# A pause behind each gather, turned orders within tiles, and column lists with more whole blocks in a four-layer graph network

## The chip, the cores and the metric

The kernel runs on one core of a Trainium2 chip. The metric is the device time of one execution in microseconds (us). The core's engines work side by side, each through its own instruction queue in order: TensorE (PE, with its weight loads PEld), VectorE (DVE), ScalarE (ACT), GpSimd (POOL) and SyncE (SP, which here only issues DMAs). DMAs that GpSimd issues go through a software queue: GpSimd itself is busy for each of them.

## The reference

Four layers over 4096 nodes with 128 features. The adjacency matrix is 4096 x 4096 and sparse: the first nodes have many neighbours (hubs), the later ones few, and the diagonal is always set. Each layer normalizes x, takes the positive part h, and adds its result to x.

```python
def layer0(h): return h @ W_self.T + (adj @ h) @ W_neigh.T + b
def layer1(h):                                    # Chebyshev, K = 3
    t1 = adj @ h
    t2 = 2.0 * (adj @ t1) - h
    return h @ w[0] + t1 @ w[1] + t2 @ w[2] + bias
def layer2(h):                                    # attention
    H = h @ weight.T
    C = (H @ att_src)[None, :] + (H @ att_dst)[:, None]
    Tau = adj.T * exp(max(0.2 * C, C))
    return (adj.T * (Tau / Tau.sum(1, keepdims=True))) @ H
def layer3(h):                                    # messages
    s, d = h @ msg_w[:, :D].T, h @ msg_w[:, D:].T
    agg = einsum('ijd,ij->id', gelu(s[:, None] + d[None, :] + msg_b), adj)
    f = gelu(concat([h, agg], -1) @ upd_w.T + upd_b) + h
    return layernorm(f) * ln_w + ln_b
for layer in (layer0, layer1, layer2, layer3):
    x = x + layer(relu(layernorm(x)))
```

## The kernel before

The nodes are put into another order on the host (lines 62 to 81), so that the 32 blocks of 128 nodes hold similar numbers of entries. The kernel then uses the sparsity in two ways.

For layers 0 to 2 the matrix is cut into stripes: `ROWS`, 16 stripes of 256 rows of the matrix, and `COLS`, 16 stripes of 256 columns (class `Stripe`, line 84). A stripe has `near` blocks, which are read whole as 128x256 tiles, and a list for the rest: those nodes outside the near blocks that have any entry in the stripe, in `cap` chunks of 128 places. Line 102 chooses how many leading blocks are near: it takes the smallest of `len(near) + cap * (1 + extra)`, with `extra` 2 for rows and 1.5 for columns (line 119). Before the change the columns have 94 near blocks and 74 chunks in all, the rows 112 and 68.

A chunk costs gathers: GpSimd DMAs with an index for each partition, all issued by the helper `gather` (lines 552 to 554). For row stripes, `Layer.gather` (line 1102) gathers for each chunk the segment of the matrix (`rseg`, in layer 0 only; it is stored to `r_tab` for the other layers) and the nodes' features (`g`, from the tables h_tab of layer 0, h_tab of layer 1's input, and u_tab). For column stripes, `fetch_columns` (line 731) gathers segments into `cseg` and SP stores them to `c_tab`, and in attention `Attention.rows` (line 1208) gathers features from `a_tab`.

The last layer works on single entries. While the matrix is read (`read_adj`, `mark`, `scan`, lines 753 to 798), VectorE picks out the words that hold entries; `entries` (line 805) turns them into lists of 158 chunks of up to 128 entries, `values` (line 930) gathers each entry's value (`e_val`), and `Messages.rows` (line 1344) gathers d's row of each entry from `d_tab` into a tile of up to four chunks (the tiles are named m, and later halves of the tiles tau and e are used too).

The order of the work is written by a planner (class `Plan`, line 255). Every part of the kernel is a generator that yields what it needs next: a buffer, an event, or an engine with a time in microseconds. The planner keeps a clock for each engine, takes the piece of work that can begin first (ranks decide between those within `PATIENCE`), and the instructions are recorded in that order. `in_order` (line 348) then fixes the order on each engine. So the times that the generators yield (`GATHER`, line 376, for a gather on GpSimd) decide the order, and not what the chip does within it. `fill` (line 604) puts matmuls on a tile of zeros into TensorE's planned gaps. Buffers are given back with `plan.release`, at the planner's time; the least time is taken first.

Attention (`Attention.attend`, line 1215) works on units of up to four blocks or chunks of a column stripe. For each block ScalarE makes a biased positive part (line 1228), for the unit one exponential (line 1231), VectorE two multiplies by the matrix tile (lines 1235 and 1237), and TensorE for each block two products: the denominators (line 1252) and the numerators (line 1254). Adds on GpSimd, besides gathers, are the bias adds of lines 979 (128x1024) and 1000 (128x512).

Of the kernel before, what the change touches and what calls it, by code (L numbers as in the profile page):

```python
# [27 lines left out]
P = 128  # L28
# [3 lines left out]
GB = BANK // D  # L32
# [83 lines left out]


RS, CS = 256, 256
R_EXTRA, C_EXTRA = 2, 1.5
TOGETHER = GB * CS // RS  # L120
ROWS = [Stripe(i, RS, R_EXTRA) for i in range(N // RS)]
COLS = [Stripe(i, CS, C_EXTRA) for i in range(N // CS)]
# [250 lines left out]


SP = "SP", 0.07
GATHER = "POOL", 1.27


def sparse_stack(tc, x, adj, adjT, diag, w_self, w_neigh, b0, w1, b1, w2, att_src, att_dst,
# [10 lines left out]
    with ExitStack() as ctx:  # L390
# [7 lines left out]
        def kept(name, shape, dtype=F32):  # L398
            return keep.tile(list(shape), dtype, name=name, tag=name)
# [149 lines left out]
        junks = tiles(keep, "junk", 2, (P, D))  # L549
        aggs = tiles(keep, "agg", 2, (P, BANK))  # L550

        def gather(dst, table, index):
            nc.gpsimd.indirect_dma_start(out=dst, out_offset=None, in_=table[:, :],  # L553
                                         in_offset=bass.IndirectOffsetOnAxis(ap=index, axis=0))


        def norm(blocks, dst):
# [24 lines left out]
        def to_features(blocks, rows):  # L582

            n = blocks.stop - blocks.start
            p = yield banks
            yield "PE", 0.42 * n
            for k in range(n):
                nc.tensor.transpose(p[:, k * P:(k + 1) * P], rows[:, k, :], ident)
            yield on_act(n * P)
            nc.scalar.copy(hT[:, blocks.start * P:blocks.stop * P], p[:, :n * P])  # L590
            plan.release(banks, p)
# [11 lines left out]

        def fill(begin, time):

            idle = min((free, i, slots.items) for slots in (banks, picks) for free, i in slots.free + [(1e9, 0)])
            if idle[0] < begin - 1.0:
                for _ in range(int(time / 0.22)):
                    nc.tensor.matmul(idle[2][idle[1]], nothing[:, :P], nothing, start=True, stop=True)  # L609
# [455 lines left out]
        class Layer:  # L1065
# [58 lines left out]
            def multiply(self):  # L1124
                for g in range(NC):
                    bank = yield accs
                    for s in ROWS:
                        if s.lo // BANK != g:
                            continue
                        acc = bank[:, s.lo % BANK:s.lo % BANK + RS]  # L1130
                        count, every = 0, len(s.near) + s.cap
                        for i, blocks in enumerate(s.tiles(TOGETHER)):
                            yield self.near_here[s.index][i]
                            t = self.at["near", s.index, i]
                            for k, b in enumerate(blocks):
                                yield self.near_done[b // GB]
                                yield on_pe(RS)
                                nc.tensor.matmul(acc, self.near[:, b, :D], as_rows(t)[:, k, :], start=count == 0,  # L1138
                                                 stop=count == every - 1)
                                count += 1  # L1140
                            plan.release(bigs, t)
                        for i, chunks in enumerate(s.groups(TOGETHER)):
                            if self.number:
                                yield self.list_here[s.index][i]
                                t = self.at["list", s.index, i]
                            for k, c in enumerate(chunks):
                                yield self.rows_here[s.index][c]
                                row = self.at["row", s.index, c]
                                if self.number:
                                    r = as_rows(t)[:, k, :]  # L1150
                                else:
                                    r, here, left = self.at["seg", s.index, c]
                                    yield here
                                yield on_pe(RS)
                                nc.tensor.matmul(acc, row[:, :D], r, start=count == 0, stop=count == every - 1)  # L1155
                                count += 1
                                plan.release(rows_g, row)
                                if not self.number:
                                    left.set(plan.finish)
                            if self.number:  # L1160
                                plan.release(bigs, t)
                    agg = yield aggs
                    yield on_act(BANK)
                    nc.scalar.copy(agg, bank)
                    plan.release(accs, bank)
                    plan.start(self.finish(g, agg), -5)
                self.through.set(plan.finish)
# [6 lines left out]
        class Attention:  # L1174
# [40 lines left out]
            def attend(self, s, a, here, blocks, chunks, rows):  # L1215
                n = len(blocks or chunks)
                yield dst_done[s.lo // BANK]
                e = yield es_
                parts = []
                for k in range(n):  # L1220
                    if blocks:
                        yield a_done[blocks[k] // GB]
                        h = hB[:, blocks[k], :]
                    else:
                        yield rows[k][1]
                        h = rows[k][0]
                    yield on_act(CS + 100)
                    nc.scalar.activation(e[:, k, :], dst[:, s.lo:s.lo + CS], AF.Relu, bias=h[:, D:D + 1])
                    parts.append(h)
                yield on_act(n * CS, "exp")  # L1230
                nc.scalar.activation(e[:, :n, :], e[:, :n, :], AF.Exp, scale=0.8)  # L1231
                yield here
                tau = yield taus
                yield on_dve(n * CS)
                nc.vector.tensor_mul(tau[:, :n, :], e[:, :n, :], a[:, :n, :])  # L1235
                yield on_dve(n * CS)
                nc.vector.tensor_mul(e[:, :n, :], tau[:, :n, :], a[:, :n, :])
                plan.release(bigs, a)
                if s.index not in self.accs:
                    self.accs[s.index] = None  # L1240
                    self.accs[s.index] = yield accs
                    self.count[s.index] = 0
                while self.accs[s.index] is None:
                    yield acc_here[s.index]
                acc_here[s.index].set(0.0)
                every = len(s.near) + s.cap
                acc = self.accs[s.index]
                yield "PE", 0.4 * (self.count[s.index] == 0) + 2 * n * 0.65
                if self.count[s.index] == 0:
                    open_bank(acc)  # L1250
                for k in range(n):
                    nc.tensor.matmul(acc[0:1, CS:2 * CS], parts[k][:, D + 1:], tau[:, k, :], start=False, stop=False)
                for k in range(n):
                    nc.tensor.matmul(acc[:, :CS], parts[k][:, :D], e[:, k, :], start=False,
                                     stop=self.count[s.index] == every - 1)
                    self.count[s.index] += 1
                plan.release(taus, tau)
                plan.release(es_, e)
                for g, _ in rows:
                    plan.release(rows_g, g)  # L1260
                if self.count[s.index] == every:
                    plan.start(finish_3(s, acc), -5)
                    self.through.set(plan.finish)
# [52 lines left out]
        class Messages:  # L1316
# [27 lines left out]
            def rows(self, u, chunks, m, here):  # L1344
                groups = -(-4 * u.cuts[-1] // BANK)
                for g in range(groups):
                    yield d_here[g]
                for q, k in enumerate(chunks):
                    yield GATHER
                    n = u.within(k)  # L1350
                    gather(m[:n, q, :], d_tab[:groups * BANK, :], e_col[:n, k:k + 1])
                    here[q].set(plan.transfer(P * D * 4))

            def prepare(self, g):
# [21 lines left out]
                nc.scalar.activation(own, own, AF.Gelu)  # L1376
                r = yield r_tiles
                yield on_dve(BANK)
                for k in range(GB):
                    nc.vector.tensor_scalar(r[:, k, :], ident, diag_sb[:, g * GB + k:g * GB + k + 1], None, op0=ALU.mult)  # L1380
                self.acc[g] = acc = yield (accs if g else picks)
                yield "PE", 4 * 0.42
# [8 lines left out]
            def message(self, g, b, u, c, chunks, m, here):  # L1391
# [4 lines left out]
                yield self.s_here[g]  # L1396
                r = yield r_tiles
                yield "DVE", 0.35 * n
                for q, k in enumerate(chunks):
                    nc.vector.tensor_scalar(r[:, q, :], iota_row[:, :P], e_row[:, k:k + 1], e_val[:, k:k + 1],  # L1400
                                            op0=ALU.is_equal, op1=ALU.mult)
                for q in range(n):
# [584 lines left out]
```

## Time and profile before

| what | us |
|---|---|
| median of 14 runs (1191.1 to 1203.62) | 1198.99 |
| the profiled execution | 1191.22 |
| its span, first to last instruction | 1189.0 |
| TensorE busy in the span | 977.6 |
| VectorE busy | 793.3 |
| GpSimd busy | 773.9 |
| ScalarE busy | 672.5 |

The mean granted clock of TensorE is 0.933 of full speed. GpSimd's 773.9 us hold 736 gathers of 1.0 us on average. The first gather starts at 83 us and the last at 1138 us. By kind, in the order in which they begin: 68 of `rseg` (83 to 347 us), 136 from `h_tab` (101 to 495), 74 of `cseg` (329 to 575), 158 of `e_val` (502 to 921), 68 from `u_tab` (533 to 663), 74 from `a_tab` (734 to 930), and 158 from `d_tab` (921 to 1139).

How to read it: rows of the timeline are start, duration, engine, line, operation, out<-in, and in brackets the time for which the engine was idle before and what ended it; "issue" stands where the profile shows no releaser. Rows by stretch give the stretch, its length, the busy time with the count of instructions in brackets, TensorE's granted clock, the share of time in which the DMA engines were busy, and GB/s. All gathers have the line of the helper `gather`, so they are told apart by their tiles.

### The profile page before, as it was taken

Reading aid. Unit: us, or ns where it says so; the run is one execution under the profiler, and the core shown is the slowest. Engines: PE = TensorE matmul, PEld = TensorE weight load, DVE = VectorE, ACT = ScalarE, POOL = GpSimd, SP = SyncE. Lnnn points to the kernel's source line nnn. Section 1 sums busy time; section 2 is a strip of 40 time slices with the busy share of each in tenths; the row PEclk is TensorE's granted clock in tenths of the full one; section 3 lists DMA queues with packets and bytes.
Section 4 is the critical chain, followed back from the end, with each engine's and each line's share of the span. In section 5 each row is a group of like instructions: output and inputs, shape, how many; then the busy total and the mean of one; then the engine's idle time right before and its main releaser. Section 6 shows DMA issues by size and latency. Waiting matters only on the chain.

```text
span 1189.0 us, 19187 instructions
## 1 busy us (share of the span) xinstructions
PE 977.6 (82%) x5943; PEld 672.9 (57%) x5943; DVE 793.3 (67%) x2982; ACT 672.5 (57%) x1344; POOL 773.9 (65%) x832
## 2 busy tenths in 40 slices
PE   5878889888788888778879788989999997779860
PEld 2545566555546766667667554554555565657650
DVE  5789978798787868658768565555555733356652
ACT  4997667777413122223456575676878632455770
POOL 5115778455366777677777777777777757777720
PEclk9978989998888999889999899899999999999995
DMA  7999999999559778898766533444455222233310
GB/s 224 378 329 334 391 386 397 382 386 368 177 160 278 233 224 268 271 280 272 220 184 194 158 90 109 117 115 114 112 132 144 66 62 54 50 69 85 75 29 21
DMA packets 175416, 236.03 MB, mean 199 GB/s; under 512 B 22453, under 2 KB 155337, under 8 KB 167113
## 3 DMA queue, kind: packets, MB, share of 16 engines
q1 hardware_dynamic: 148904, 186.45, 46.3%
q0 software_dynamic: 26400, 48.27, 16.6%
q8 instruction: 49, 0.80, 0.3%
q14 instruction: 63, 0.51, 0.1%
HBM read 203.41 MB, written 31.23 MB: 197 GB/s over the span
## 4 chain that ended last, share of the span: by engine, by line
DMA 26%; PE 26%; DVE 16%; ACT 14%; POOL 9%; issue 7%; SPq 0%; POOLq 0%; DVEq 0%; ACTq 0%
POOL e_val L553 5%; PE acc L1138 5%; ACT mask L768 3%; DMA big<-in_adjT 3%; DMA dst<-in_adj 3%; DMA g<-h_tab,fetch_row 3%; ACT junk L568 3%; PE acc L1155 3%; DMA m<-d_tab,e_col 2%; DMA cseg<-in_adj,seg_col 2%; DMA e_val<-in_adj,e_at 2%; PE pick L609 2%; POOL g L553 2%; DMA g<-a_tab,fetch_col 2%; PE bank L597 2%
## 5 line engine op out<-in xcount | busy, mean ns | idle before, releaser
L553 POOL DMA_INDIRECT e_val<-in_adj,e_at x158 | 158.3, 1002 | 48.0 <-issue 41.3
L553 POOL DMA_INDIRECT g<-h_tab,fetch_row x136 | 134.3, 987 | 44.0 <-issue 27.3
L609 PE MATMUL pick<-nothing 128*128 128x512 f16 x532 | 135.4, 401 | 0.0
L609 PEld LDWEIGHTS <-nothing 128*128 128x128 f16 x795 | 80.5, 104 | 88.0 <-issue 17.6
L1138 PE MATMUL acc<-big,hA 128*128 128x256 f32 x448 | 119.1, 411 | 7.9 <-DMA big<-in_adjT 6.5
L553 POOL DMA_INDIRECT rseg<-in_adjT,seg_row x68 | 73.7, 1084 | 66.5 <-issue 35.0
L1138 PEld LDWEIGHTS acc<-big,hA 128*128 128x128 f32 x448 | 88.6, 207 | 22.8 <-DMA big<-in_adjT 7.7
L553 POOL DMA_INDIRECT cseg<-in_adj,seg_col x74 | 70.8, 957 | 42.0 <-issue 19.5
L553 POOL DMA_INDIRECT g<-a_tab,fetch_col x74 | 78.2, 1057 | 22.6 <-issue 14.3
L768 ACT ACTIVATE mask<-dst 128x2048 fp8e4<-128x2048 f32 x43 | 81.9, 1904 | 19.0 <-DMA dst<-in_adj 19.0
L1235 DVE TENSOR_TENSOR tau<-e,big 128x512 f32<-128x512 f32 (+3 forms) x61 | 54.3, 890 | 43.5 <-ACT e L1231 41.3
L553 POOL DMA_INDIRECT m<-d_tab,e_col x70 | 69.0, 986 | 21.3 <-issue 14.0
L553 POOL DMA_INDIRECT tau<-d_tab,e_col x63 | 61.2, 972 | 28.9 <-issue 12.2
L1155 PE MATMUL acc<-big,g 128*128 128x256 f32 x272 | 73.0, 402 | 8.2 <-DMA big<-r_tab 5.0
L553 POOL DMA_INDIRECT g<-u_tab,fetch_row x68 | 64.5, 948 | 20.7 <-issue 10.7
L1138 PE MATMUL acc<-big,hB 128*128 128x256 f32 x224 | 64.8, 430 | 13.9 <-DMA big<-in_adjT 13.9
L568 ACT ACTIVATE junk<-xN,stat 128x128 f32<-128x128 f32 x128 | 51.3, 401 | 41.9 <-DVE stat L564 29.5
L887 ACT COPY ehit<-pick 128x192 f32<-128x192 f32 (+7 forms) x74 | 20.3, 287 | 88.5 <-PE pick L884 75.2
L609 PE MATMUL bank<-nothing 128*128 128x512 f16 x263 | 67.4, 399 | 0.0
L1155 PE MATMUL acc<-rseg,g 128*128 128x256 f32 x136 | 44.1, 426 | 27.2 <-DMA g<-h_tab,fetch_row 27.0
L890 DVE SCALAR_TENSOR_TENSOR ehit<-ehit,pos,pick 128x32 f32<-128x32 f32 (+7 forms) x158 | 38.7, 284 | 39.1 <-ACT ehit L887 38.8
L622 ACT ACTIVATE sel_t<-iota_row,mids 128x512 f32<-128x512 f32 (+3 forms) x43 | 27.1, 641 | 60.7 <-DVE mids L617 60.1
(328 smaller groups left out, 2606.4 us busy)
## 6 DMA issues: line engine op xcount, KB each, us to landing
dst<-in_adj SPq DMA_DIRECT2D x43, 1024.0 KB
big<-in_adjT SPq DMA_DIRECT2D x45, 512.0 KB
raw<-in_adj SPq DMA_DIRECT2D x21, 1024.0 KB
big<-in_adjT SPq DMA_DIRECT2D x66, 256.0 KB
big<-r_tab SPq DMA_DIRECT2D x30, 512.0 KB
c_tab<-cseg SPq DMA_DIRECT2D x74, 128.0 KB
r_tab<-rseg SPq DMA_DIRECT2D x68, 128.0 KB
big<-c_tab SPq DMA_DIRECT2D x15, 512.0 KB
```

The costliest lines, as they stand in the source:

```text
L553: nc.gpsimd.indirect_dma_start(out=dst, out_offset=None, in_=table[:, :], in_offset=bass.IndirectOffsetOnAxis(ap=index, axis=0))
L568: nc.scalar.activation(junk, src[:, k, :], AF.Square, bias=st[:, 0, k:k + 1], accum_out=st[:, 1, k:k + 1])
L597: nc.tensor.matmul(p[:, k * D:(k + 1) * D], lhs[:, k * P:(k + 1) * P], w, start=i == 0, stop=i == len(terms) - 1)
L609: nc.tensor.matmul(idle[2][idle[1]], nothing[:, :P], nothing, start=True, stop=True)
L622: nc.scalar.activation(lane["t"][:, :n * P], iota_row[:, :n * P], AF.Abs, bias=mids[:, g:g + 1])
L768: nc.scalar.activation(mask[:, h * HALF:(h + 1) * HALF], raw_of[b, h], AF.Sigmoid, scale=1e38, accum_out=marks[:, 2 * b + h:2 * b + h + 1] ...
L887: nc.scalar.copy(hit, pv[:, :, :W])
L890: nc.vector.scalar_tensor_tensor(hit[:, q, :], hit[:, q, :], pos0[:, k + q:k + q + 1], pv[:, q, W:2 * W], op0=ALU.is_le, op1=ALU.mult, acc ...
L1138: nc.tensor.matmul(acc, self.near[:, b, :D], as_rows(t)[:, k, :], start=count == 0, stop=count == every - 1)
L1155: nc.tensor.matmul(acc, row[:, :D], r, start=count == 0, stop=count == every - 1)
L1235: nc.vector.tensor_mul(tau[:, :n, :], e[:, :n, :], a[:, :n, :])
```

## The change

It has four parts.

- Behind each gather, GpSimd adds the tile of ones to itself into a tile `pause` of 128x128 f32, which nothing reads. The planner's time for a gather goes from 1.27 to 1.52.
- `C_EXTRA` goes from 1.5 to 3. The columns then have 156 near blocks and 56 chunks (94 and 74 before): the first two stripes are whole (32 blocks each), the third has 10 blocks and 5 chunks, the others up to 11 blocks and 3 or 4 chunks. The rows are the same. With it 700 gathers remain of 736.
- Several loops over the parts of a tile run backwards: the transposes of four blocks in `to_features`, the attention products of a unit, the gathers of a message tile, and the making of the r tiles. Row buffers of a group are given back at the group's end, and in another order.
- `fill` compares only the first two members of its entries.

The planner runs with the new times and lists, so the order of the instructions differs on every engine from the first hundred on. In the sparse part TensorE has 6605 instructions shown for 6418, of them 881 idle-time matmuls for 811.

```diff
-R_EXTRA, C_EXTRA = 2, 1.5
+R_EXTRA, C_EXTRA = 2, 3
...
-GATHER = "POOL", 1.27
+GATHER = "POOL", 1.52
...
+        pause = kept("pause", (P, P))
+
         def gather(dst, table, index):
+
             nc.gpsimd.indirect_dma_start(out=dst, out_offset=None, in_=table[:, :],
                                          in_offset=bass.IndirectOffsetOnAxis(ap=index, axis=0))
+            nc.gpsimd.tensor_add(pause, ones, ones)
...
-            for k in range(n):
+            for k in reversed(range(n)):
                 nc.tensor.transpose(p[:, k * P:(k + 1) * P], rows[:, k, :], ident)
...
-            idle = min((free, i, slots.items) for slots in (banks, picks) for free, i in slots.free + [(1e9, 0)])
+            idle = min(((free, i, slots.items) for slots in (banks, picks) for free, i in slots.free + [(1e9, 0)]),
+                       key=lambda slot: slot[:2])
...
                                 count += 1
-                                plan.release(rows_g, row)
                                 if not self.number:
                                     left.set(plan.finish)
+                            for k, c in enumerate(reversed(chunks)):
+                                plan.release(rows_g, self.at["row", s.index, c], plan.finish + 1e-6 * k)
...
-                for k in range(n):
+                for k in reversed(range(n)):
                     nc.tensor.matmul(acc[0:1, CS:2 * CS], parts[k][:, D + 1:], tau[:, k, :], start=False, stop=False)
-                for k in range(n):
+                for k in reversed(range(n)):
                     nc.tensor.matmul(acc[:, :CS], parts[k][:, :D], e[:, k, :], start=False,
                                      stop=self.count[s.index] == every - 1)
...
-                for g, _ in rows:
-                    plan.release(rows_g, g)
+                for k, (g, _) in enumerate(rows):
+                    plan.release(rows_g, g, plan.finish + 1e-6 * k)
...
-                for q, k in enumerate(chunks):
+                for q, k in reversed(list(enumerate(chunks))):
                     yield GATHER
                     n = u.within(k)
                     gather(m[:n, q, :], d_tab[:groups * BANK, :], e_col[:n, k:k + 1])
...
-                for k in range(GB):
+                for k in reversed(range(GB)):
                     nc.vector.tensor_scalar(r[:, k, :], ident, diag_sb[:, g * GB + k:g * GB + k + 1], None, op0=ALU.mult)
...
-                for q, k in enumerate(chunks):
+                for q, k in reversed(list(enumerate(chunks))):
                     nc.vector.tensor_scalar(r[:, q, :], iota_row[:, :P], e_row[:, k:k + 1], e_val[:, k:k + 1],
                                             op0=ALU.is_equal, op1=ALU.mult)
```

## The prediction

> **What bounds the kernel now.** I read the shares of the span first, then the busy time of each engine by stretch, then GpSimd's instructions one after another, then what GpSimd waits for. The shares alone would send a reader to TensorE:
>
> ```profile
> PE 977.6 (82%) x5943; PEld 672.9 (57%) x5943; DVE 793.3 (67%) x2982; ACT 672.5 (57%) x1344; POOL 773.9 (65%) x832
> ```
>
> But TensorE's time holds the idle-time matmuls of line 609 (135.4 and 67.4 us in the groups), and GpSimd's 65% leaves out what lies between its instructions. The timeline of GpSimd from 176 to 184 us, each row start, duration, line, operation and the idle time before it:
>
> ```profile
> 176.31 0.94 POOL L553 DMA_INDIRECT g<-h_tab,fetch_row  x1 [0.30 <-issue]
> 177.56 0.95 POOL L553 DMA_INDIRECT rseg<-in_adjT,seg_row  x1 [0.30 <-PE acc L1155]
> 178.81 0.94 POOL L553 DMA_INDIRECT g<-h_tab,fetch_row  x1 [0.30 <-issue]
> 179.77 1.28 POOL L1000 TENSOR_TENSOR xN<-xN,b_sb 128x512 f32<-128x512 f32 x1
> 181.21 1.77 POOL L553 DMA_INDIRECT rseg<-in_adjT,seg_row  x1 [0.16 <-DMA rseg<-in_adjT,seg_row]
> 183.28 0.94 POOL L553 DMA_INDIRECT g<-h_tab,fetch_row  x1 [0.30 <-issue]
> ```
>
> A gather is busy 0.94 us and then 0.30 us pass, whatever is named as releaser: gathers queued back to back start every 1.25 us. So 0.30 us belongs to each gather as much as its busy time does. The rows of line 553 alone, in five stretches (us, busy time, count, clock, DMA):
>
> ```profile
> 83.00:216.00 133.00, 84.74 (x80) 0.94 1.01 376
> 216.00:347.00 131.00, 62.73 (x61) 0.88 0.85 299
> 347.00:664.00 317.00, 231.18 (x244) 0.94 0.81 238
> 664.00:963.00 299.00, 221.81 (x216) 0.97 0.41 111
> 963.00:1140.00 177.00, 134.43 (x137) 0.98 0.28 66
> ```
>
> From 347 to 1140 us there are 597 gathers, 587 us busy (0.984 each). With 597 x 0.30 = 179 us that is 766 of 793 us; the idle time beyond 0.30 us, added up from the timeline, is 21 us. GpSimd is full for two thirds of the span, and the last gather starts at 1138; what follows (50 us to 1189) is the last block's message, normalization and checks. Before 347 us it is not full: from 216 to 347 it idles 46 us beyond the 0.30, from 83 to 216 some 12. The waits from 347 us on say the same; only the d_tab row and the c_tab rows are real waits:
>
> ```profile
> POOL tau L553 <- DMA d_tab<-agg: 10.0, 1, 10.0
> POOL cseg L553 <- DMA c_tab<-cseg: 9.1, 9, 2.1
> ```
>
> **The pause.** Each gather is followed by an add of 128x128 f32. There is no such row, so I bound it by the two adds of the same kind: 128x1024 at a median of 2353 ns (line 979), 128x512 at 1276 ns (line 1000). The line through them is 2.10 ns an element and 199 ns fixed, so 128 elements take 0.47 us; in proportion to the shorter row it would be 1276 / 4 = 0.32 us, which is the lower end. A 128x128 memset took 0.20 us (line 446) and bounds it from below further off. I take 0.46, since the two rows demand a fixed part. What is around it: the add above starts 0.02 us after the gather ends, and the gather behind it starts 0.16 us after the add. So the pause replaces a gap of 0.30 by 0.46 + 0.16: +0.32 us a gather (+0.18 at the lower end). The pair of gathers at 178.81 and 181.21 confirms it: 2.40 us apart in place of 1.25, so a 1.28 us add cost 1.15, 0.13 less than its length, and 0.46 - 0.13 is 0.33. A gain is excluded unless the gap of 0.30 shrinks by more than the add takes. The pause waits for a count of GpSimd's own, that of the pause before it, finished a gather earlier: nothing. Queued behind each pause is the next gather, and behind that ScalarE's bias activations, TensorE's message matmuls and, with e_val, VectorE's multiplies.
>
> **Fewer chunks.** Column chunks fall from 74 to 56. Each is gathered twice (cseg, then a_tab's rows), so 36 gathers go and 700 stay: 36 x 1.284 = 46 us less of GpSimd's time, all behind 329 us, where the first cseg stands. In their place 62 blocks are read whole, so attention has 212 block units for 168: 44 more. From the groups between 664 and 963 us, a unit on TensorE costs (51.7 + 47.9) / 94 = 1.06 us (each product is two rows), 47 us in all; on ScalarE 0.50 and a share of the exponential (46.1 / 168 = 0.27), 34 us; on VectorE two multiplies of 0.31, 27 us. What covers them is the longer GpSimd stretch. The changed program's order has 204 gathers between the last of u_tab and the first message into a tau buffer, which with the price below last 327 us. TensorE is busy 274 of 299 us there now, 33 of it idle-time matmuls, so some 241 + 47 = 288; ScalarE 217 + 34 = 251; VectorE 173 + 27 = 200. All fit, TensorE with 39 us to spare. If that cover were gone (a pause at nothing, 204 x 1.284 = 262 us) TensorE would set this stage, 26 us above it. The first two stripes are now 64 units without a gather, while 58 e_val gathers stand on GpSimd: neither waits for the other. On SP, 18 c_tab stores go and the loads change little (484 instructions for 500); bytes stay about even (62 loads of 128 KB in, 18 x 3 transfers of 128 KB out), with the DMA share at 0.41.
>
> **Turned orders.** Transposes taken from the last block wait for the last normalized block: at most three transposes of 0.31 us later, on chains whose next step is a wait for gathers. Reversed reads within a message cost nothing, since its first product reads all four parts. The r tiles made in reverse delay the first product by up to 3 x 0.35 us; the gathers' landing (2.5 to 4 us in the chain of waits) covers it. The reversed attention matmuls wait for one multiply that covers all blocks. Row buffers given back last chunk first can hold a gather by up to three chunk products, 3 x 0.8 us; 14 buffers cover it, as they do now, where these waits are the 0.30 rows. I cost all of these at nothing; without cover they would be some 1 us for each of 16 groups of a layer or stripe, 15 us at most.
>
> **VectorE beside the pause.** The rows show that an add on GpSimd and work on VectorE hold each other up. VectorE's timeline from 50 to 56 us and from 178 to 183 us; GpSimd's adds run at 51.49 (2.74 us, median 2.35) and 179.77:
>
> ```profile
> 50.80 1.22 DVE L788 TENSOR_TENSOR words<-mask,spread 128x1024 int32<-128x1024 int32 x1
> 52.05 3.27 DVE L790 SCALAR_TENSOR_TENSOR words<-mask,words 128x1024 f32<-128x1024 f32 x1
> ```
>
> ```profile
> 179.49 2.65 DVE L788 TENSOR_TENSOR words<-mask,spread 128x1024 int32<-128x1024 int32 x1
> 182.17 1.23 DVE L790 SCALAR_TENSOR_TENSOR words<-mask,words 128x1024 f32<-128x1024 f32 x1
> ```
>
> Lines 790 and 788 take 1.22 us when no add is beside them. Of the 12 adds, two were longer, by 0.39 and 0.28 us: 0.056 each on average. So 0 to 0.06 us a pause on GpSimd; I take 0 and keep 0.06. The Trainium skill speaks against this change here ("SBUF — State Buffer", Who interferes with whom): a VectorE instruction with two SBUF inputs and a GpSimd instruction that reads SBUF exclude each other for a whole instruction, and the later one waits. By that rule every pause that meets such an instruction is longer, and the sum would be near 1356, the forecast with 31 us more.
>
> **The sum.** From 347 us: 561 gathers x (0.984 + 0.46 + 0.16) = 900 us, in place of 766: +134. Of the 21 us of waits some 10 are used up by the lateness: -10. Before 347 us, 141 pauses ask 45 us. The first 80 come in a full stretch and make GpSimd 26 us late at 216; the 46 us of idle time behind that take these 26 and the 20 of the other 61, if the lists come no later. VectorE makes the lists and is busy 225 of 264 us there, so I leave +10 (0 to 30). In all +134 on the profiled execution's 1191.2: 1325 us. The median of the runs shown is 1199, 8 us over the profiled one; the range takes that in.
>
> **The rivals.** *A cheap pause*: 0.32 us, as proportion would have it. 561 x 1.464 = 821, +55, and attention lasts 204 x 1.464 = 299 us with TensorE at 288, nearly touching, +5: 1191 + 55 - 10 + 10 + 5, about 1250. For it: rows on GpSimd are rough; against it: the fixed part in both adds. Chance 0.20. *Pause and VectorE in each other's way*: 561 x 0.056 = 31 us, and in the lists' stage 141 pauses hold VectorE for 0.46 us nearly half the time (seven of the 12 adds had a held VectorE instruction), 29 us against 39 of slack there, +10: 1365. Chance 0.20. *Faster*: the pause lies wholly inside the 0.30 us, so that GpSimd keeps 1.284 a gather. Then the 36 gathers are 46 us of gain and TensorE gives 26 back in attention: 1191 - 46 + 26, about 1171. It decides from a net price below 46 / 561 = 0.08 us a gather (less with TensorE's 26 us). Against it is the gather pair 2.40 us apart. Chance 0.04. *No change* (a net price just there, or pauses filling only idle time): 1191 to 1199, chance 0.01; GpSimd has 21 us idle for 180 us of pauses.
>
> **The numbers.** The forecast has 0.55, from 1285 to 1345. The range takes in half of the cheap pause and most of the disturbed one: 1262 to 1372. About 0.3% is what a measurement of this kernel can tell from no change. Faster 0.04, same 0.01, slower 0.95.
>
> **What would show it.** The pause as a group of 700 with a mean near 0.46 us; gathers 1.56 us apart where they are undisturbed (0.94 + 0.46 + 0.16); GpSimd busy over 1000 us in all; the last gather at about 1275 us with 50 us behind it; attention's TensorE rows (its two products) at 212 units and no wait for them on GpSimd. The forecast is wrong if pauses start while the gather before is still counted, if gathers with a pause ahead are shorter than 0.94, or if TensorE is full between the last u_tab gather and the messages.

## The result, and the profile after

| | median, us | profiled execution | span |
|---|---|---|---|
| before (47 runs beside the changed kernel's) | 1197.08 | 1191.22 | 1189.0 |
| after (10 runs, 1361.01 to 1373.81) | 1366.28 | 1366.41 | 1364.3 |

The ratio is 1.1416, with a 95% interval of [1.1389, 1.1443]. The forecast of 1325 us had the direction, the bound and most of the size; 41 us are missing from it: the time lies outside 1285 to 1345, to which the forecast gave 0.55, and where the rival of a pause and VectorE in each other's way put it (1365, chance 0.20).

From the page of the changed kernel: the busy times of the span, and two of its costliest groups.

```profile
PE 1077.3 (79%) x6167; PEld 720.6 (53%) x6167; DVE 899.9 (66%) x2933; ACT 699.9 (51%) x1385; POOL 1100.5 (81%) x1496
L558 POOL TENSOR_TENSOR pause<-ones 128x128 f32<-128x128 f32 x700 | 325.8, 465 | 13.4
L556 POOL DMA_INDIRECT e_val<-in_adj,e_at x158 | 183.3, 1160 | 25.0 <-issue 24.0
```

GpSimd went from 773.9 to 1100.5 us busy, of which the 700 pauses are 325.8, 0.465 us each. But the gathers became dearer too: those of e_val from 1002 to 1160 ns. VectorE is 107 us busier (793.3 to 899.9); the forecast gave it 27 us of work (without the pause it is at 809).

The gathers alone (line 556), then the pauses alone (line 558), in the changed kernel's stages: the making of the lists, the layers, attention, messages. Columns are the stretch, its length, the busy time with its count, TensorE's clock, DMA share, GB/s.

```profile
84.00:378.00 294.00, 153.30 (x139) 0.87 0.88 302
378.00:712.00 334.00, 203.76 (x212) 0.92 0.72 211
712.00:1070.00 358.00, 222.05 (x192) 0.93 0.37 102
1070.00:1326.00 256.00, 157.53 (x158) 0.93 0.22 55
```

```profile
84.00:378.00 294.00, 65.61 (x138) 0.87 0.88 302
378.00:712.00 334.00, 89.44 (x212) 0.92 0.72 211
712.00:1070.00 358.00, 100.08 (x192) 0.93 0.37 102
1070.00:1326.00 256.00, 70.29 (x158) 0.93 0.22 55
```

The last rseg gather ends at 378 us (347 before), and from there 562 gathers follow to 1326 us. Their busy time is 583 us (1.038 each, 0.984 before), the pauses' 260 (0.462 each), and 562 gaps of 0.16 are 90: 933 of 948 us. In attention a gather takes 1.16 us and its pause 0.52; in the messages 1.00 and 0.44. Where nothing is beside it, the timeline of GpSimd in the changed kernel looks like this:

```profile
899.21 0.96 POOL L556 DMA_INDIRECT e_val<-in_adj,e_at  x1 [0.16 <-issue]
900.19 0.41 POOL L558 TENSOR_TENSOR pause<-ones 128x128 f32<-128x128 f32 x1
900.76 0.96 POOL L556 DMA_INDIRECT e_val<-in_adj,e_at  x1 [0.16 <-issue]
901.74 0.41 POOL L558 TENSOR_TENSOR pause<-ones 128x128 f32<-128x128 f32 x1
```

The pause stands right behind the gather, takes 0.41 us, and 0.16 us later the next gather starts: 1.55 us from gather to gather for 1.25, the median of all spacings. Attention in the same kernel, GpSimd and then VectorE:

```profile
753.06 1.77 POOL L556 DMA_INDIRECT e_val<-in_adj,e_at  x1 [0.16 <-issue]
754.85 1.11 POOL L558 TENSOR_TENSOR pause<-ones 128x128 f32<-128x128 f32 x1
756.11 1.76 POOL L556 DMA_INDIRECT e_val<-in_adj,e_at  x1 [0.16 <-issue]
757.90 0.66 POOL L558 TENSOR_TENSOR pause<-ones 128x128 f32<-128x128 f32 x1
758.71 1.76 POOL L556 DMA_INDIRECT e_val<-in_adj,e_at  x1 [0.15 <-issue]
```

```profile
754.32 1.39 DVE L1243 TENSOR_TENSOR e<-tau,big 128x1024 f32<-128x1024 f32 x1
755.63 1.42 DVE L1241 TENSOR_TENSOR tau<-e,big 128x1024 f32<-128x1024 f32 x1
757.08 1.22 DVE L1243 TENSOR_TENSOR e<-tau,big 128x1024 f32<-128x1024 f32 x1
758.22 1.42 DVE L1241 TENSOR_TENSOR tau<-e,big 128x1024 f32<-128x1024 f32 x1
```

Here the two engines go in step. The pause at 754.85 ends at 755.96, 0.25 us after VectorE's multiply ends (755.71). VectorE's next multiply ends at 757.05; the gather that began beside it ends 0.82 us later, at 757.87. It goes on so: the next pause ends at 758.56, after the multiply that ends at 758.30, and the next gather at 760.47, 0.83 us after the one that ends at 759.64. Gather to gather is 2.6 to 3.1 us.

### The profile page after: what moved, and what is told of

Its sections match the earlier page's. It is cut to its first block, busy times and chain, and to the rows that moved or that the text cites. A ratio compares the mean times of both kernels' runs of the same rounds, so it can differ in the third digit from the quotient of the medians.

```text
span 1364.3 us, 20122 instructions
## 1 busy us (share of the span) xinstructions
PE 1077.3 (79%) x6167; PEld 720.6 (53%) x6167; DVE 899.9 (66%) x2933; ACT 699.9 (51%) x1385; POOL 1100.5 (81%) x1496
## 4 chain that ended last, share of the span: by engine, by line
POOL 35%; DVE 21%; PE 18%; DMA 12%; ACT 7%; issue 6%; POOLq 0%; SPq 0%; DVEq 0%; ACTq 0%
POOL pause L558 11%; POOL e_val L556 10%; DMA g<-h_tab,fetch_row 4%; POOL g L556 4%; POOL tau L556 4%; PE acc L1143 3%; POOL m L556 3%; PE acc L1160 3%; PE pick L614 2%; PE bank L601 2%; POOL rseg L556 2%; ACT junk L572 2%; DMA dst<-in_adj 1%; DMA m<-d_tab,e_col 1%; ACT mask L773 1%
## 5 line engine op out<-in xcount | busy, mean ns | idle before, releaser
L558 POOL TENSOR_TENSOR pause<-ones 128x128 f32<-128x128 f32 x700 | 325.8, 465 | 13.4
L556 POOL DMA_INDIRECT e_val<-in_adj,e_at x158 | 183.3, 1160 | 25.0 <-issue 24.0
L614 PE MATMUL bank<-nothing 128*128 128x512 f16 x350 | 94.6, 410 | 0.0
L1241 DVE TENSOR_TENSOR tau<-e,big 128x1024 f32<-128x1024 f32 (+2 forms) x66 | 69.6, 1054 | 36.0 <-ACT e L1237 34.9
L1258 PE MATMUL acc<-tau,hB 128*1 128x256 f32 x312 | 81.4, 400 | 12.4 <-DVE tau L1241 12.4
L556 POOL DMA_INDIRECT tau<-d_tab,e_col x77 | 77.1, 1001 | 12.3 <-issue 10.3
L1260 PE MATMUL acc<-e,hB 128*128 128x256 f32 x312 | 83.8, 406 | 0.3 <-DVE e L1243 0.3
L1234 ACT ACTIVATE e<-dst,hB 128x256 f32<-128x256 f32 x156 | 68.9, 495 | 9.7 <-PE acc L1260 9.7
L1260 PEld LDWEIGHTS acc<-e,hB 128*128 128x128 f32 x312 | 57.0, 196 | 31.0 <-issue 14.0
L1243 DVE TENSOR_TENSOR e<-tau,big 128x1024 f32<-128x1024 f32 (+2 forms) x66 | 70.7, 1071 | 2.1
```

The costliest lines, as they stand in the source:

```text
L558: nc.gpsimd.tensor_add(pause, ones, ones)
```

## The experiments

Each ratio is to runs of the kernel before on the same chip, which had medians of 1195.7 to 1197.3 us, but for the last.

**The pause alone, in the order of before.**

```diff
+        pause = kept("pause", (P, P))
...
             nc.gpsimd.indirect_dma_start(out=dst, out_offset=None, in_=table[:, :],
                                          in_offset=bass.IndirectOffsetOnAxis(ap=index, axis=0))
+            nc.gpsimd.tensor_add(pause, ones, ones)
```

> The kernel before with the pause alone, and the order of before. Theory, the pause is the whole loss and more: from 347 us on, 597 gathers, each dearer by what the changed kernel's rows show (pause 0.466 mean, gather 0.055 longer, 0.16 for the gap of 0.30: 0.38 us), 227 us, and some 30 us in the lists' stage, less 10 to 20 us of waits: 1410 to 1440 us, above the changed kernel by about 36 gathers x 1.68 = 60 us. Rival, the turned orders and the whole blocks carry a good part of the 173 us: under 1340 us.

Measured 1441.73 us, ratio 1.2055 [1.1995, 1.2114], just above the theory's range. The pause is the whole loss and more; 736 of them cost 246 us, 0.33 each. The rest of the change, taken together, is a gain.

**The changed kernel without the pause.**

```diff
-            nc.gpsimd.tensor_add(pause, ones, ones)
```

> The changed kernel without the pause; order, lists and planner's time as changed. Theory: 36 gathers fewer give 46 us on GpSimd and TensorE, nearly full in attention then, gives some back: 1160 to 1185 us, faster than before. Rival, whole blocks and turned orders cost time: 1200 us or more.

Measured 1157.64 us, ratio 0.9691 [0.9636, 0.9746]: 38 us faster than before, and just below the theory's range. In this order the 700 pauses cost 1366.28 - 1157.64 = 209 us, 0.30 each.

**A memset in place of the add**: nearly as long on GpSimd, but it reads nothing.

```diff
-        pause = kept("pause", (P, P))
+        pause = kept("pause", (P, 320))
...
-            nc.gpsimd.tensor_add(pause, ones, ones)
+            nc.gpsimd.memset(pause, 0.0)
```

> The changed kernel with a memset of 128x320 in place of the add: by the memset rows some 0.37 us, near the 0.41 of an undisturbed pause, but nothing is read. Theory, VectorE and the pause hold each other up over reads: pauses have no long ones, the mean gather falls from 1.05 back to 1.00, VectorE from 900 to about 830 us busy, the span to 1364 - 28 (shorter pauses) - 38 (long pauses) - 38 (long gathers), about 1260 to 1300 us. Rival, only GpSimd's time counts and what is read makes no difference: 1364 - 28, about 1335 us.

Measured 1291.75 us, ratio 1.0810 [1.0756, 1.0864], in the range of the theory. Two groups of its GpSimd rows:

```profile
L558 POOL MEMSET pause<- 128x320 f32 x700 | 277.2, 396 | 0.4
L556 POOL DMA_INDIRECT e_val<-in_adj,e_at x158 | 175.8, 1113 | 25.7 <-issue 24.7
```

The memset is 0.38 us undisturbed and 0.396 on average; the add was 0.41 and 0.465. So the undisturbed times differ by 700 x 0.03 = 21 us, and the kernels by 75. The other 54 us go with reading, the main thing in which the two differ: pauses are held up less (0.016 for 0.055 each, 27 us), and the gathers take 713 us in all for 737. Beside attention's two multiplies the 68 memsets took 0.38 us each, as undisturbed, and 54 adds 0.81 on average. The gathers do not fall all the way back: without a pause they take 700 us, so 13 of the 37 us that the add costs them come with a pause that reads nothing as well. VectorE fell only to 870 us, not to 830: the memset and VectorE hold each other up too, elsewhere. Of the 71 memsets over 0.42 us, 56 stand beside VectorE's instructions of line 629, which read one whole tile. That part of the expectation was wrong.

**The pause cut to one column.**

```diff
-            nc.gpsimd.tensor_add(pause, ones, ones)
+            nc.gpsimd.tensor_add(pause[:, 0:1], ones[:, 0:1], ones[:, 0:1])
```

> The changed kernel with the pause cut to one column (128x1), same place, same order. The line of the prediction has 0.199 us fixed, which with 0.16 behind it is 0.06 more than the gap of 0.30 a gather: 700 x 0.06 = 42 us over the kernel without a pause (1157.64), 1180 to 1205 us. The rows after the change (0.41 for 128, 1.27 for 512 columns, undisturbed) have 0.12 fixed: 0.02 less than the gap, 1145 to 1165 us. Rival, any instruction between two gathers costs its own price whatever its length: over 1240 us.

Measured 1238.60 us, ratio 1.0346 [1.0300, 1.0392]: 81 us over the kernel without a pause, above the expectations from either line and just below the rival's. Undisturbed it takes 0.20 us, the 0.199 of the forecast's line, and gathers are then 1.33 to 1.34 us apart for 1.25: 700 x 0.09 = 63 us. The mean pause is 0.268, though, and the gathers are as long as with the full pause (737 us in all, 700 without one). GpSimd, then VectorE:

```profile
708.13 1.90 POOL L556 DMA_INDIRECT e_val<-in_adj,e_at  x1
710.04 0.34 POOL L558 TENSOR_TENSOR pause<-ones 128x1 f32<-128x1 f32 x1
710.52 1.89 POOL L556 DMA_INDIRECT e_val<-in_adj,e_at  x1
712.44 0.33 POOL L558 TENSOR_TENSOR pause<-ones 128x1 f32<-128x1 f32 x1
```

```profile
707.97 1.23 DVE L1243 TENSOR_TENSOR e<-tau,big 128x1024 f32<-128x1024 f32 x1
709.11 1.22 DVE L1241 TENSOR_TENSOR tau<-e,big 128x1024 f32<-128x1024 f32 x1
710.36 1.22 DVE L1243 TENSOR_TENSOR e<-tau,big 128x1024 f32<-128x1024 f32 x1
711.50 1.22 DVE L1241 TENSOR_TENSOR tau<-e,big 128x1024 f32<-128x1024 f32 x1
```

Even an add of one column ends 0.05 us after a multiply does (710.33 and 710.38, 712.72 and 712.77), and the gather that follows at 710.52 meets the next multiply (710.36 to 711.58) at its beginning and ends 0.83 us after it. VectorE is hardly held by this pause: 810 us busy, 809 without one. So the dear gathers don't need a VectorE that was held before. What makes them dear is where they start: with a pause just behind the beginning of a multiply, without one anywhere beside it. Counted over the gathers that begin beside one of these multiplies (those of 0.6 us or more, up to 0.05 us before their end): without a pause 87, begun at a median of 0.75 us into the multiply and 1.18 us long on average; with one column 50, at 0.16 us and 1.77 long; with the memset 57, at 0.20 and 1.47; with the full pause 57, at 0.37 and 1.62.

**Whole blocks alone**, in the kernel before.

```diff
-R_EXTRA, C_EXTRA = 2, 1.5
+R_EXTRA, C_EXTRA = 2, 3
```

> The kernel before with C_EXTRA = 3 alone (56 column chunks for 74, 156 whole blocks for 94). Theory: 36 gathers x 1.284 = 46 us less on GpSimd, partly given back by TensorE in attention: 1160 to 1185 us. Rival, the added block work sets attention: 1197 us or more.

Measured 1217.72 us, ratio 1.0195 [1.0148, 1.0242]: slower, as the rival had it, with the same lists that are 38 us faster in the changed kernel without its pause. What GpSimd waited for between 820 and 1000 us:

```profile
POOL m L553 <- PE acc L1252: 21.4, 2, 21.1
POOL g L553 <- PE acc L1254: 16.4, 6, 7.2
POOL e L553 <- PE acc L1254: 16.2, 1, 16.2
POOL e L553 <- DMA d_tab<-agg: 15.9, 1, 15.9
```

The planner's order for these lists has e_val earlier: its last gather is the 499th here and the 574th in the kernel before, and GpSimd was through with it at 821 us. Until attention's last products began, at 962 us, the gathers left to it had to wait, mostly for attention's products: between 820 and 1000 us it idled 73 us beyond the 0.30 of each gather, in the kernel before 10. Three runs then asked what the changed kernel has against this.

**The planner's figure alone**, in the kernel before.

```diff
-GATHER = "POOL", 1.27
+GATHER = "POOL", 1.52
```

> The kernel before with the planner's time for a gather at 1.52 alone: not an instruction more, another order. Two runs speak of it: whole blocks alone took 1217.72 us, the changed kernel without the pause 1157.64, and between them lie only this figure and the turned orders. Theory, the figure makes the planner put the gathers that others wait for ahead of e_val (u_tab's were done at 639 us against 663) and is most of the 60 us: 1160 to 1185 us. Rival, the turned orders are: 1190 to 1205 us.

Measured 1211.12 us, ratio 1.0130 [1.0081, 1.0179]: slower, by itself, and above both expectations. Only 4 e_val gathers stand ahead of the last u_tab gather here (37 in the kernel before), and between 348 and 640 us GpSimd idles 33 us beyond the 0.30 of each gather, for 11.

**The turned orders alone**, with the release order and `fill` as changed.

```diff
-            for k in range(n):
+            for k in reversed(range(n)):
                 nc.tensor.transpose(p[:, k * P:(k + 1) * P], rows[:, k, :], ident)
...
```

> The kernel before with the turned orders alone. Theory: nothing, since their covers stand, 1190 to 1205 us. Rival, they carry part of the 60 us between whole blocks alone and the changed kernel without the pause: under 1180 us.

Measured 1203.00 us, ratio 1.0053 [1.0028, 1.0078]: some 6 us slower, in the theory's range, though the theory put the cost at nothing; the 15 us of the forecast's worst case allow it.

**Whole blocks and the figure, orders not turned.**

```diff
-R_EXTRA, C_EXTRA = 2, 1.5
+R_EXTRA, C_EXTRA = 2, 3
...
-GATHER = "POOL", 1.27
+GATHER = "POOL", 1.52
```

> Whole blocks and the planner's 1.52, orders not turned, no pause. Theory, the figure of 1.52 is what the whole blocks lacked: 1150 to 1170 us, as the changed kernel without the pause (1157.64). Rival, the turned orders are needed: 1195 to 1220 us.

Measured 1156.39 us, ratio 0.9654 [0.9597, 0.9711]: the fastest kernel of the study, and the same as with turned orders (0.9691). Line 553's gathers in three stretches, whole blocks alone and then whole blocks with the figure:

```profile
640.00:820.00 180.00, 137.12 (x135) 0.96 0.46 132
820.00:1000.00 180.00, 82.49 (x81) 0.98 0.40 112
1000.00:1160.00 160.00, 119.34 (x121) 0.98 0.28 67
```

```profile
640.00:820.00 180.00, 137.98 (x133) 1.00 0.51 145
820.00:1000.00 180.00, 128.48 (x129) 1.00 0.33 87
1000.00:1160.00 160.00, 87.95 (x89) 0.89 0.23 57
```

From 820 to 1000 us, 129 gathers for 81: the hole is closed (13 us of idle time beyond the 0.30 for 73). With the figure of 1.52, 21 e_val gathers stand ahead of the last u_tab gather in the order, with 1.27 it is 54; u_tab ends at 636 us for 664, attention's last product begins at 909 for 962, and e_val lasts to 905 us for 821.

**Whole blocks and turned orders with the planner's 1.27**, as an edit of the changed kernel.

```diff
-GATHER = "POOL", 1.52
+GATHER = "POOL", 1.27
...
-            nc.gpsimd.tensor_add(pause, ones, ones)
```

> Whole blocks and turned orders with the planner's 1.27, no pause. Theory, without the 1.52 the whole blocks lose as they did alone: 1205 to 1225 us. Rival, the turned orders repair it: 1155 to 1185 us.

Measured 1205.74 us, ratio 1.0076 [1.0042, 1.0110]: turned orders repair little. GpSimd is through with e_val at 817 us and idles 74 us beyond the 0.30 between 820 and 1000 us, as with whole blocks alone. The gain of the changed kernel's other parts needs whole blocks and the figure together; each alone loses.

**Whole blocks, 1.27, and e_val held back.**

```diff
         def values():
+            yield layers[2].through
             for number, group in enumerate(GROUPS):
```

> Whole blocks with the planner's 1.27, straight orders, no pause, and one line more: the e_val gathers wait in the plan until layer 2 is through. In the run with whole blocks alone (1217.72 us) e_val was done at 821 us, the last u_tab gather was late (663 against 636 with the planner's 1.52), and GpSimd then idled 77 us until attention's end. Theory, that order of e_val is why 1.27 loses: with e_val behind u_tab, u_tab ends by 640 us, GpSimd has e_val left through attention, and the time is 1145 to 1170 us, as with 1.52 (1156.39). Rival, something else in the plan of 1.52 matters (buffers, TensorE's order): 1190 us or more.

Measured 1197.60 us, ratio 1.0006 [0.9978, 1.0033]: 20 us of the 61, and the expectation failed. u_tab ended at 639 us and GpSimd had e_val until 948, as meant; but with e_val gone from layer 2 it idled there instead: first 13.7 us at 527 us for the table itself, then between u_tab gathers that wait for TensorE to free their buffers. Beyond the 0.30 of each gather it idled 48 us between 348 and 640 us (7 with whole blocks alone), and nothing between 820 and 1000 (73). So the order of e_val is a part of the answer: e_val has to fill both holes.

**Whole blocks for the rows as well**, in the kernel before, without a pause.

```diff
-R_EXTRA, C_EXTRA = 2, 1.5
+R_EXTRA, C_EXTRA = 3, 3
...
-GATHER = "POOL", 1.27
+GATHER = "POOL", 1.52
```

> Whole blocks for the rows as well (R_EXTRA = 3: 156 near blocks and 56 chunks for 112 and 68), C_EXTRA = 3, planner's 1.52, no pause. If GpSimd still bounds the layers, 48 gathers fewer are 60 us: 1100 to 1125 us. Rival, TensorE (44 blocks x 3 layers x 0.82 us = 108 us more) and the loads (17 MB more) take its place in the layers: 1165 us or more.

Measured 1168.20 us, ratio 0.9767 [0.9711, 0.9823]: 48 gathers fewer, and yet behind whole columns alone (0.9654), as the rival had it. What it costs is more than the gathers it saves, and the rival's two causes, TensorE's products and the loads, were not told apart. The trace shows a third: 64 e_val gathers stand ahead of the last u_tab gather (21 with whole columns alone), e_val ends at 824 us, and GpSimd again idles 62 us beyond the 0.30 between 820 and 1000 us (13). The hole of whole blocks alone is back.

**The figure at 1.40**, with whole blocks.

```diff
-R_EXTRA, C_EXTRA = 2, 1.5
+R_EXTRA, C_EXTRA = 2, 3
...
-GATHER = "POOL", 1.27
+GATHER = "POOL", 1.40
```

> Whole blocks, straight orders, no pause, and the planner's time for a gather at 1.40, between 1.27 (1217.72 us) and 1.52 (1156.39 us). In the order it makes, 31 e_val gathers stand ahead of the last u_tab gather (54 with 1.27, 21 with 1.52) and the last e_val is the 531st gather (499th and 542nd). Theory, the time follows what GpSimd waits for, which follows that order: 1160 to 1185 us, with 95 to 115 us of waits beyond the 0.30 (148.8 and 88.4). Rival, the plan is a lottery and the order of e_val does not tell: anywhere from 1150 to 1220 us, with no tie to that order.

This run does not decide between the two: on its chip the kernel before itself took 1508.04 us, and this one 1524.07, ratio 1.0173 [1.0060, 1.0287], with TensorE's granted clock at 0.82 to 0.84 in both (0.91 to 0.93 for the kernel before elsewhere). How the time moves between 1.27 and 1.52 stays open.

## Why the prediction was right, and where its sizes were off

What GpSimd spends on gathers and pauses, busy and idle ahead of them, can be added up for each kernel from its groups:

| kernel | gathers and pauses, busy | idle ahead | sum | span | rest |
|---|---|---|---|---|---|
| before | 734.8 | 301.6 | 1036 | 1189 | 153 |
| after | 1062.6 | 160.3 | 1223 | 1364 | 141 |
| after without the pause | 699.9 | 305.7 | 1006 | 1158 | 152 |
| after with the memset | 990.6 | 159.7 | 1150 | 1291 | 141 |
| after with one column | 924.9 | 168.2 | 1093 | 1239 | 145 |
| pause alone | 1094.2 | 195.2 | 1289 | 1440 | 151 |
| whole blocks alone | 693.0 | 360.4 | 1053 | 1215 | 162 |
| whole blocks, 1.52 | 702.1 | 300.5 | 1003 | 1154 | 151 |

The sum counts idle time too, so it comes near the span whatever sets the pace; the rest is mainly what lies before the first gather and behind the last. What tells is how it splits. With the pause GpSimd has 363 us more of busy time than without it and 145 us less of idle time, and the span is 206 us longer; behind the lists gathers, pauses and their gaps are 933 of 948 us. So there GpSimd sets the pace of the changed kernel, as the prediction's first step has it. Without a pause it does so only while it has work that waits for nothing: whole blocks alone took 42 us of busy time off it and put 59 us of idle time in.

*The pause, 0.46 and 0.16 for a gap of 0.30.* Right in sum: 0.462 on average behind the lists, 0.16 behind it, no gap ahead of it. It was composed otherwise: 0.41 undisturbed and 0.05 of holding up by VectorE, where the prediction had 0.46 undisturbed and kept 0.06 aside. That its two errors of 0.05 cancel is luck. The cheap pause (0.32) is out; so is the faster rival, since even one column costs 81 us.

*Gathers stay at 0.984.* This term was mis-sized: 1.038 behind the lists, 562 x 0.054 = 30 us. Some 11 of these are that a gather with nothing beside it takes 0.96 us behind a pause and 0.94 without one; the rest are gathers held up by VectorE. The prediction looked at what a pause and VectorE do to each other, and not at the gather behind the pause, although one stands in its own rows: the gather at 181.21, behind an add, takes 1.77 us and ends 0.84 us after line 788's instruction (179.49 + 2.65). The rival had its 31 us from the pause instead, and put 10 us more into the lists, where 21 more were measured; that its 1365 is met is chance. All pauses make gathers dearer: the add and the one column by 37 us in all, the memset by 13.

*The lists, +10.* Measured 31 (378 us for 347). Without the pause this order ends them at 353, with the memset at 364: 25 us are the pause's. With the memset 14 of these go, but with one column, which reads, 15 do (363), so reading is not shown to be the cause. The prediction's reason for the term, VectorE held in the stage where it is busiest, fits but was not tested by itself; its size was too small.

*The waits, -10, and what follows the last gather.* From 378 us the sum of gathers, pauses and gaps leaves 15 us, with the few adds and memsets in it: about the 10 that the prediction left. The end after the last gather is 38 us for 50, which nobody forecast. It goes with the order and not with the pause: 38 to 39 in all five kernels that have whole columns and 1.52 with the rows as before, and 50 to 52 in the kernel before, with the pause alone and with turned orders alone; why stays open. The three differences, 31 behind the lists, 21 in them and -12 at the end, make 40 of the 41 us between 1325 and the profiled 1366.41.

*Fewer chunks, 46 us less and covered.* Here the working failed although the number came out. The prediction has 1191 - 46 + 26 = 1171 for the changed kernel whose pause costs nothing, and the run without the pause took 1157.64. But by the same working the lists alone would win, and they lose 22 us. The prediction counted gathers off GpSimd's queue and asked only if TensorE fits under it; it gave no price to the planner's figure, as if the order of the queue would stay. What an emptier queue is worth depends on what is left in it when attention runs: e_val gathers, here 158 of them.

*Turned orders, nothing.* Alone 6 us at a measured 0.5%; with whole blocks and the figure of 1.52 nothing that the runs can tell (0.9691 and 0.9654). Under a pause they were not tried by themselves. Which of the loops costs the 6 us was not tried.

## What to carry to other kernels

Count the gap behind each instruction of a queue to its load: GpSimd at 65% busy was full for two thirds of the span, and 700 pauses, less the gaps they replaced, came out as 209 us of time. Price an added instruction with its neighbours: the one behind it, and the other engine that holds it up. Where a planner orders a full queue, work that nothing waits for yet belongs beside the stages that would starve it: taking 36 gathers away lost 22 us in one order and won 41 in another.

## What the runs showed of the hardware

A gather on GpSimd that begins beside a long VectorE instruction with two SBUF inputs is held until about 0.83 us after that instruction's end: 1.76 to 1.90 us for 0.95 in the rows above. Of the 57 such gathers beside attention's multiplies in the changed kernel, 56 end 0.79 to 0.85 us behind them. In the kernel before, the 33 gathers that began beside the multiply of line 1235 took 1.31 us on average, and 18 beside the reduction of line 783, which reads one tile, 0.94, none over 0.96. The Trainium skill ("SBUF — State Buffer", Who interferes with whom) states the exclusion of such an instruction and a GpSimd instruction that reads, which the pauses follow in the main (0.81 us on average beside the multiplies, for 0.41, and memsets, which only write, 0.38 as ever); that a tensor_tensor does not stall a DMA issued by GpSimd, as it has it from a probe, is not what these gathers show. Theirs are indirect, with an index tile in SBUF; plain ones were not tried.

TensorE's granted clock fell with the pause: 0.950 without it in the changed kernel, 0.906 with it, 0.851 with the pause in the kernel before. Behind the lists GpSimd's 933 of 948 us leave it little to cost; for the stage of the lists nothing here tells whether it cost time.
